# A two-layer table-lookup convolution block on one core: first layer without softmax maxima, lookup over 18 stacks, weights normalised in transposed form, PSUM banks in pairs

## The chip, the cores and the metric

The kernel runs on one core of a Trainium2 chip, in one launch, in fp32 throughout. The metric is device microseconds of one execution; lower is better. The engines are TensorE (PE), VectorE (DVE), ScalarE (ACT), GpSimd (POOL) and SyncE (SP, which only issues DMAs here). Each runs its instructions in the order in which they stand and waits for the others through semaphores.

## The reference

For x of shape (16, 256, 28, 28), a block of pre-activation form is computed. A convolution is replaced here by a soft lookup: each 3x3 patch of a channel (9 numbers) is compared with the channel's 16 centroids, and a softmax over the 16 gives the weights of the centroids' rows in a table.

```python
def amm_conv3x3(x, centroids, w_sub):            # (C,16,9), (C,9,O)
    p = patches(x)                               # B, C, 9 -> p: (b, n, c, 9)
    d = sum(p*p) - 2*einsum('bncs,cks->bnck', p, centroids) + sum(centroids**2)
    attn = softmax(-d, axis=-1)                  # over the 16 centroids
    lut = einsum('cks,cso->cko', centroids, w_sub)
    return einsum('bnck,cko->bno', attn, lut)    # summed over c and k
def block(x):
    out = relu(bn1(amm_conv3x3(x, centroids1, w_sub1)))
    out = bn2(amm_conv3x3(out, centroids2, w_sub2))
    out = se_layer(out)                          # mean over pixels, two small products, sigmoid gate
    return relu(out + x)
y = x + block(groupnorm(x, 32 groups))
```

## The kernel before

**Layout.** The 256 channels are put into 88 rows of 3; 4 such rows fill the 128 partitions of a *stack* (32 partitions each: 27 patch numbers, a row of ones, rows for the maxima), so a layer has 22 stacks (NT), taken in 11 groups of two (NG). The 784 pixels are two tiles of 384 and 400. Layer 1 or 2 of one image is a *stage* of 22 *slots* (11 groups x 2 tiles), and the 32 stages run in the order (1,0) (1,1) (2,0) (1,2) (2,1) ..., so that a stage of layer 1 and one of layer 2 alternate and an image's layer 1 is done a stage ahead of its layer 2. In the code the layers are l = 0 and 1.

**What one group goes through.** Patches of nine shifted copies (`pat`, in DRAM) are loaded to `pt` (L344). PE forms the logits (`lg`, L357: 8 products of 31 rows by 64 columns); DVE transposes them in 32x32 blocks into `z` (L373, 4 banks) and takes the maximum over the 16 centroids (`mx`, L381); for each unit of two groups the maxima are transposed (`mt`, L390) and go through DRAM (`dm`, SP's queue) into spare rows of `pt`. PE then forms the logits a second time, with the maxima subtracted by the product (L357 again), ACT takes the exponential (`e`, L422), and PE multiplies by the centroids (`nm`, L431), which gives the numerators, 9 weighted numbers per channel, and the softmax's sum as one more row. ACT copies these to `q` (L443) and makes 1/sum as exp(-ln(sum)) (`r`, L450 and L451); DVE spreads it to the 9 rows by a stream shuffle (`rb`, L466), POOL multiplies (L467), and PE does the lookup, `q` times the table's rows into two accumulators `acc` of 128 output channels (L475), over all 22 stacks.

**Around it.** When the accumulators of a tile are full, ACT applies the batch norm and writes the layer's image (L491) or `y` (L501). From an image three DRAM copies (`home`, shifted by one column for dx = 0 and 2, with `side` as the shifted image in SBUF, copied by POOL, L271) are written, and from these nine DMAs fill `pat` (L280); all of these are POOL's. A new image is loaded to `xt`, its group statistics are taken on DVE (L222), and POOL normalises it (L253). An image is closed by the gate (two small products, ACT L313 and DVE L316 to L321) and the two halves of `finish` (ACT L330, DVE L331 and L332).

**What sets the order.** Nothing reorders: the program order is written by hand. `at(slot, pos, f, ...)` notes a step, and the steps are emitted sorted by slot, then position 0 to 9. So each engine's order is that of the steps below.

```python
at(s, 0, a_logits, u, gi); at(s, 1, a_turn, u, gi); at(s, 8, a_max, u, gi)
at(s + LB, 5, b_logits, u, gi); at(s + LB, 6, b_exp, u, gi)      # LB = 4
at(s + LN, 3, b_num, u, gi);    at(s + LN, 4, b_keep, u, gi)     # LN = 5
at(s + LN + 1, 0, r_make, u, gi); at(s + LC - 1, 7, c_scale, u, gi)
at(s + LC, 2, c_look, u, gi, 0);  at(s + LC, 7, c_look, u, gi, 1)  # LC = 7
```

PSUM has two accumulator banks and a ring of six single banks (`bank`), each of them [128, 512] fp32, used in turn for logits, numerators and the small products.

Of the kernel before, what the change touches and what calls it, by code (L numbers as in the profile page):

```python
# [15 lines left out]
P = 128  # L16
# [3 lines left out]
K = 16  # L20
NCH = 3
NRT = 88
NT = NRT // 4
NG = NT // 2
CPAD = NRT * NCH
GN_EPS = 1e-5
BN_EPS = 1e-5

# [6 lines left out]
NROW = [r for r in range(32) if r % 8 != 7][:27]  # L35

PXT = ((0, 384, 0, 384), (384, 400, 368, 416))
UNITS = ((0, 2), (2, 2), (4, 2), (6, 2), (8, 2), (10, 1))  # L40


def prow(j, s):
    base, step = PROW[j * 3 + s % 3]
    return base + step * (s // 3)


@with_exitstack
def kernel(
# [11 lines left out]
    sums: bass.AP,  # L61
# [5 lines left out]
):  # L67

# [17 lines left out]
    p_ring = ctx.enter_context(tc.tile_pool(name="p_ring", bufs=6, space=PSUM))  # L86
# [5 lines left out]
    def bank(name):  # L92
        return p_ring.tile([P, 512], F32, tag="ps", name=name)
# [5 lines left out]

    DX = CPAD * NPAD  # L100
    d_home = [dram.tile([3 * CPAD, NPAD], F32, name=f"home{i}") for i in range(2)]
    d_pat = [dram.tile([NRT * 32, HW], F32, name=f"pat{i}") for i in range(3)]
    d_zero = dram.tile([2, NPAD], F32, name="zero")
# [3 lines left out]
    xpool = ctx.enter_context(tc.tile_pool(name="xpool", bufs=2))  # L107

    def load_x(b):
        t = xpool.tile([P, NB, HW], F32, tag="xt", name="xt")  # L110
        nc.gpsimd.dma_start(t, x[b].rearrange("(b p) n -> p b n", p=P))
        xs[b] = t

    xs = {}
    load_x(0)

    def zeros(dims):
        return view(d_zero, 0, dims)  # L120

    def clear_home(i):
        t = d_home[i]
        nc.scalar.dma_start(view(t, 0, [[NPAD, 3 * CPAD], [29 * W, 2], [1, W]]), zeros([[0, 3 * CPAD], [0, 2], [1, W]]))
        nc.scalar.dma_start(view(t, C * NPAD, [[DX, 3], [NPAD, CPAD - C], [1, NPAD]]), zeros([[0, 3], [0, CPAD - C], [1, NPAD]]))

    def clear_pat(i):
        t = d_pat[i]
        nc.scalar.dma_start(view(t, 7 * HW, [[32 * HW, NRT], [8 * HW, 4], [1, HW]]), zeros([[0, NRT], [0, 4], [1, HW]]))
        nc.scalar.dma_start(view(t, ONE * HW, [[32 * HW, NRT], [1, HW]]), view(d_zero, NPAD, [[0, NRT], [1, HW]]))  # L130

    with tc.tile_pool(name="zo", bufs=1) as zpool:
        zo = zpool.tile([2, NPAD], F32, name="zo")
        nc.vector.memset(zo, 1.0)
        nc.vector.memset(zo[0:1], 0.0)
        nc.scalar.dma_start(d_zero, zo)
    clear_home(0)
    clear_pat(0)


    nc.vector.tensor_scalar_mul(gmat, gmat, 1.0 / 8.0)
    mhalf = const.tile([P, NB], F32, name="mhalf")
    nc.vector.memset(mhalf, -0.5)
# [19 lines left out]
    nc.sync.dma_start(b1_sb, se_b1.rearrange("(p o) -> p o", o=1))  # L163
    nb2_sb = const.tile([P, NB], F32, name="nb2_sb")
# [10 lines left out]
    for l in range(2):  # L175
        ga, be, mu, va = (vecs[:, :, 4 * l + i] for i in range(4))
        sc = const.tile([P, NB], F32, name=f"bnsc{l}")
        sh = const.tile([P, NB], F32, name=f"bnsh{l}")
        rsqrt(sc, va, BN_EPS, NB)
        nc.vector.tensor_mul(sc, sc, ga)  # L180
        nc.vector.tensor_mul(sh, mu, sc)
        nc.vector.tensor_sub(sh, be, sh)
        bn.append((sc, sh))


    def setup_codes(l):
        wf = wd[l].rearrange("p t m -> p (t m)")
        n = NT * 64
        for c0 in range(0, n, 416):
            m = min(416, n - c0)  # L190
            sq = tpool.tile([P, 416], F32, tag="z", name="sq")
            nc.gpsimd.tensor_tensor(sq[:, :m], wf[:, c0 : c0 + m], wf[:, c0 : c0 + m], ALU.mult)  # L192
# [12 lines left out]
    for t in mxs:  # L205
        nc.vector.memset(t, 0.0)

    sides = {dx: const.tile([P, NB, HW], F32, name=f"side{dx}") for dx in (0, 2)}
    for t in sides.values():
        nc.gpsimd.memset(t, 0.0)  # L210
# [444 lines left out]
```

## Time and profile before

| | |
|---|---|
| three runs | 4280.79, 4292.75, 4295.6 us (median 4292.75) |
| the profiled execution's own time | 4305.45 us, span 4303.8 us |
| busy, share of the span | PE 95%, DVE 87%, ACT 72%, POOL 52% |
| chain that ended last, by engine | PE 84%, DMA 7%, POOL 4%, DVE 3% |
| DMA | 744.32 MB in 563718 packets, mean 173 GB/s |
| TensorE clock granted | 0.984 |

The profile lists, for the one execution that the hardware profiler recorded, the busy time of each engine, then groups of equal instructions with their total, the mean duration in ns of one, and what ended the idle time ahead of them ("<-PE lg L357": a product of line 357 was waited for). The duration of one instruction includes the time from its start until its result is there, so instructions that follow each other on one engine start closer together than their durations say. 704 slots in the span make some 5.5 to 6 us for each. "The chain that ended last" follows the waits back from the last instruction.

### The profile page before, as it was taken

To read this page: it belongs to the slowest core of one execution; us is meant where nothing else is said; L and a number is where in the kernel's file an instruction comes from. 1 tells how busy PE (TensorE), PEld (TensorE's weight loads), DVE (VectorE), ACT (ScalarE), POOL (GpSimd) and SP (SyncE) were. 2 spreads that over 40 slices of the span, in tenths; PEclk is the share of its full clock that TensorE was granted. 3 is DMA by queue.
4 is the path that set the end of the run, shared out by engine and by line. 5 is a ranking of instruction groups with operands and counts; after the bars stand their busy time and mean duration, and the time that the engine had idled before them with its cause. 6 is when DMAs were issued, how large, how long until landed. Compare 5 with 4: busy or idle time off the path is not lost.

```text
span 4303.8 us, 104911 instructions
## 1 busy us (share of the span) xinstructions
PE 4069.6 (95%) x39696; PEld 1481.4 (34%) x39696; DVE 3761.5 (87%) x9144; ACT 3109.7 (72%) x5905; POOL 2252.7 (52%) x2436
## 2 busy tenths in 40 slices
PE   0899999999999999999999999999999999999998
PEld 0333333333333333333333333333333333333333
DVE  0888998889989989888999989989898889989896
ACT  0467777777777777777777777777777777777677
POOL 2455545555464655545555465554545555455443
PEclk9999999999999999999999999999999999999999
DMA  6654655646465564655646456563655646556532
GB/s 210 207 175 120 209 166 182 191 140 218 132 198 186 181 199 122 197 159 184 199 128 211 151 187 192 171 211 103 209 175 187 193 126 209 159 183 198 168 113 65
DMA packets 563718, 744.32 MB, mean 173 GB/s; under 512 B 419490, under 2 KB 443186, under 8 KB 562956
## 3 DMA queue, kind: packets, MB, share of 16 engines
q0 software_dynamic: 149248, 642.59, 44.3%
q1 hardware_dynamic: 409328, 90.35, 10.1%
q8 instruction: 313, 5.13, 0.5%
q10 hardware_dynamic: 4636, 4.66, 0.4%
q14 instruction: 193, 1.58, 0.1%
HBM read 601.26 MB, written 379.15 MB: 228 GB/s over the span
## 4 chain that ended last, share of the span: by engine, by line
PE 84%; DMA 7%; POOL 4%; DVE 3%; issue 1%; ACT 1%; SPq 0%; ACTq 0%; POOLq 0%; DVEq 0%
PE acc L475 45%; PE lg L357 27%; PE nm L431 12%; DMA dm<-mt 2%; POOL xt L253 2%; DMA pt<-dm 2%; DVE z L373 1%; DMA pat<-home 1%; DMA home<-zero 1%; POOL q L467 1%; DVE mx L381 1%; POOL side L269 1%; ACT e L422 0%; DVE rb L466 0%; DVE y L331 0%
## 5 line engine op out<-in xcount | busy, mean ns | idle before, releaser
L467 POOL TENSOR_TENSOR q<-q,rb 128x384 f32<-128x384 f32 (+1 forms) x1408 | 1404.6, 1015 | 1922.8 <-DVE rb L466 1922.7
L475 PE MATMUL acc<-q,ws 128*128 128x384 f32 (+1 forms) x5632 | 2257.8, 524 | 45.5 <-POOL q L467 44.8
L373 DVE STREAM_TRANSPOSE z<-lg 128x416 f32<-128x416 f32 (+1 forms) x2816 | 1436.8, 568 | 367.8 <-PE lg L357 361.5
L357 PE MATMUL lg<-pt,wd 31*64 31x384 f32 (+2 forms) x22528 | 1392.7, 524 | 98.9 <-DMA pt<-dm 47.3
L475 PEld LDWEIGHTS acc<-q,ws 128*128 128x128 f32 x5632 | 961.2, 190 | 1331.0 <-issue 794.2
L381 DVE TENSOR_REDUCE mx<-z 128x26 f32<-128x416 f32 (+1 forms) x2816 | 1396.9, 561 | 0.0
L422 ACT ACTIVATE e<-lg 128x400 f32<-128x400 f32 (+1 forms) x2816 | 1192.0, 523 | 213.7 <-PE lg L357 212.9
L443 ACT COPY q<-nm 128x384 f32<-128x384 f32 (+1 forms) x1408 | 615.4, 489 | 911.5 <-PE nm L431 904.0
L466 DVE STREAM_SHUFFLE rb<-r 128x384 f32<-128x384 f32 (+1 forms) x1408 | 773.5, 597 | 0.3 <-issue 0.2
L450 ACT ACTIVATE r<-q,srow 128x768 f32<-128x768 f32 (+1 forms) x704 | 755.9, 1074 | 0.0
L357 PEld LDWEIGHTS lg<-pt,wd 31*64 31x64 f32 x22528 | 362.1, 131 | 971.4 <-DVE z L373 480.2
L431 PE MATMUL nm<-e,cw 64*32 64x384 f32 (+1 forms) x11264 | 632.8, 506 | 0.0
L451 ACT ACTIVATE r<-r 128x768 f32<-128x768 f32 (+1 forms) x704 | 603.2, 857 | 22.4
L344 POOL DMA_DIRECT2D pt<-pat x384 | 300.8, 783 | 32.9 <-DMA pat<-home 32.9
L280 POOL DMA_DIRECT2D pat<-home x288 | 245.7, 853 | 37.4 <-DMA pat<-zero 29.3
L431 PEld LDWEIGHTS nm<-e,cw 64*32 64x32 f32 x11264 | 128.0, 105 | 397.9 <-ACT r L451 323.5
L390 DVE STREAM_TRANSPOSE mt<-mx 128x256 f32<-128x256 f32 (+1 forms) x384 | 162.5, 423 | 13.2
L253 POOL TENSOR_SCALAR xt<-xt,gn_gm,gn_rstd 128x784 f32<-128x784 f32 x32 | 95.4, 2984 | 0.1
L194 PE MATMUL sqp<-sq,nhalf_sb 128*128 128x416 f32 (+1 forms) x16 | 9.8, 789 | 62.4 <-POOL sq L192 62.4
L331 DVE SCALAR_TENSOR_TENSOR y<-xt,gn_rstd,y 128x784 f32<-128x784 f32 x32 | 33.2, 1036 | 39.1 <-ACT y L330 38.6
L195 DVE TENSOR_TENSOR wd<-wd,sqp 128x416 f32<-128x416 f32 (+1 forms) x8 | 4.0, 521 | 68.0 <-DMA srow<-in_sums 61.0
L501 ACT ACTIVATE y<-acc,bnsh,bnsc 128x384 f32<-128x384 f32 (+1 forms) x64 | 44.4, 694 | 15.7 <-PE acc L475 15.7
(59 smaller groups left out, 514.7 us busy)
## 6 DMA issues: line engine op xcount, KB each, us to landing
pat<-home POOLq DMA_DIRECT2D x288, 808.5 KB, 6.4
pt<-pat POOLq DMA_DIRECT2D x160, 832.0 KB, 7.7
pt<-pat POOLq DMA_DIRECT2D x160, 768.0 KB, 5.1
home<-side POOLq DMA_DIRECT2D x64, 784.0 KB, 4.2
dm<-mt SPq DMA_DIRECT2D x640, 64.0 KB, 4.2
xt<-in_x POOLq DMA_DIRECT2D x32, 784.0 KB, 6.7
pt<-dm SPq DMA_DIRECT2D x320, 50.0 KB
pt<-dm SPq DMA_DIRECT2D x320, 48.0 KB
```

The lines of the kernel that those rows point to most:

```text
L344: nc.gpsimd.dma_start(pt[:, : 2 * ng, :wn], view(pat_of(u["l"], u["b"]), 2 * g0 * P * HW + wpx, [[HW, P], [P * HW, 2 * ng], [1, wn]]),)
L357: nc.tensor.matmul(bs[i][64 * h : 64 * h + 64, :n], lhsT=wd[l][32 * i : 32 * i + rows, 2 * g + h, :], rhs=u["pt"][32 * i : 32 * i + rows, ...
L373: nc.vector.transpose(z[:, :n], u["lg", gi][i][:, :n])
L381: nc.vector.tensor_reduce(u["mx"][:, 4 * gi + i].rearrange("p (c b) -> p b c", c=2)[:, : n // 32], z[:, :n].rearrange("p (b c k) -> p b c ...
L422: nc.scalar.activation(e[:, :n], bk[:, :n], AF.Exp, scale=2.0)
L431: nc.tensor.matmul(bs[h][32 * i : 32 * i + 32, :n], lhsT=cw[l][64 * h : 64 * h + 64, g, i, :], rhs=e[64 * h : 64 * h + 64, :n], start=True ...
L443: nc.scalar.copy(q[:, h * n : (h + 1) * n], bk[:, :n])
L450: nc.scalar.activation(r[:, : 2 * n], u["q", gi][:, : 2 * n], AF.Ln, scale=srow[:, 0:1], bias=srow[:, 1:2])
L451: nc.scalar.activation(r[:, : 2 * n], r[:, : 2 * n], AF.Exp, scale=-1.0)
L466: nc.vector.stream_shuffle(rb[:, :n], r[:, v], MASK)
L467: nc.gpsimd.tensor_tensor(q[:, v], q[:, v], rb[:, :n], ALU.mult)
L475: nc.tensor.matmul(accs[key][:, :n], lhsT=ws[l][:, 2 * g + h, o * P : (o + 1) * P], rhs=u["q", gi][:, h * n : (h + 1) * n], start=(g == 0 ...
```

## The change

Seven things change together.

1. **Layer 1 without maxima.** Its groups have no first logits, no `z`, `mx`, `mt`, `dm`: the second logits stand alone, with the maxima's rows of `pt` at zero. In return two reductions a group (`ext`, L473 and L474) keep the largest sum and the largest 1/sum; at the end of the program they are compared with a limit of 1e26, the result is read into a register, and behind a branch stands a loop over the images that computes everything again with maxima.
2. **18 stacks in the lookup.** Channel number rt + 84 j stands in row rt, column j. The two groups that come first in a tile (9 and 10, by ORDER) put their weighted numbers, 90 rows, into `qx`; ACT copies five of these per stack into the rows of the sums of the other nine groups (L490), so that the lookup has 36 products of 128 rows in a tile instead of 44, spread over 11 slots by LOOKS.
3. **Normalisation in transposed form.** DVE transposes the numerators from PSUM to `nt` (pixels on the partitions, L466), takes the reciprocal of the three sums per 32 columns (`rc`, L470), POOL multiplies with `rc` read nine times each (L487, L501), and DVE transposes back to `q` (L511). The copies L443, the logarithm and exponential L450 and L451 and the shuffle L466 go.
4. **Paired banks.** Three pairs of banks in turn in place of six banks; transposes, maxima and exponentials each work on a pair, so half as many instructions of twice the size. 400 pixels are transposed as 416 columns each.
5. **No `home`.** Images lie in SBUF with a padding row above and below (`im`, `side`), and 15 smaller DMAs fill `pat` from there in a stage. They are issued by ACT, not POOL.
6. **Moved steps.** Side copies from POOL to ACT (L289, L291), normalisation of the new image from POOL to DVE (L281). One `xt` buffer instead of two; `load_x` one slot ahead of `gn_stats` instead of two; LB 5 (was 4), LC 5 (was 7).
7. **Set-up.** Zeros and ones come as an input instead of being made and written to DRAM, the first image's work comes ahead of the second layer's set-up.

```diff
+    ring = [p_ring.tile([P, 2, 512], F32, name=f"pair{i}") for i in range(3)]
+    def pair():
+        turn[0] += 1
+        return ring[turn[0] % 3]
-    xpool = ctx.enter_context(tc.tile_pool(name="xpool", bufs=2))
+    xpool = ctx.enter_context(tc.tile_pool(name="xpool", bufs=1))
...
     def gn_apply(b):
-            nc.gpsimd.tensor_scalar(
-                xt[:, k], xt[:, k], gm[:, k, 0:1], rstd[:, k : k + 1], op0=ALU.subtract, op1=ALU.mult
+            nc.vector.tensor_scalar(
+                ims[0][:, k, W : W + HW], xt[:, k], gm[:, k, 0:1], rstd[:, k : k + 1], op0=ALU.subtract, op1=ALU.mult
...
-            nc.gpsimd.tensor_copy(to[:, :, 1:W], img[:, :, 0 : W - 1])
+            nc.scalar.copy(to[:, :, 1:W], img[:, :, 0 : W - 1])
...
+    PIECES = [(0, 0, 0, 84, 0), (1, 0, 84, 44, 0), (1, 1, 0, 40, 44), (2, 1, 40, 84, 0), (0, 1, 124, 4, 84)]
+    def to_pat(l, i, pat):
+        dx, (j, k, p0, n, rt) = (1, 0, 2)[i // len(PIECES)], PIECES[i % len(PIECES)]
+        v = (ims[l] if dx == 1 else sides[dx])[p0 : p0 + n, k]
+        nc.scalar.dma_start(
+            view(pat, (32 * rt + base) * HW, [[32 * HW, n], [step * HW, 3], [1, HW]]),
+            bass.AP(v.tensor, v.offset, [list(v.ap[0]), [W, 3], [1, HW]]),
...
     def a_turn(u, gi):
-        for i in range(4):
-            nc.vector.transpose(z[:, :n], u["lg", gi][i][:, :n])
+        for ps in u.pop(("lg", gi)):
+            nc.vector.transpose(z[:, : 64 * nb].rearrange("p (i m) -> p i m", i=2), ps[:, :, : 32 * nb])
...
     def b_exp(u, gi):
-        for bk in u.pop(("lg", gi)):
-            nc.scalar.activation(e[:, :n], bk[:, :n], AF.Exp, scale=2.0)
+        for ps in u.pop(("lg", gi)):
+            nc.scalar.activation(e[:, :, :n], ps[:, :, :n], AF.Exp, scale=2.0)
...
+    def b_turn(u, gi):
+        t = npool.tile([P, 26, 32], F32, tag="nt", name="nt")
+        nc.vector.transpose(
+            t[:, : 2 * nb].rearrange("p (h b) r -> p h (b r)", h=2), u.pop(("nm", gi))[:, :, : 32 * nb])
+        nc.vector.reciprocal(rc[:, : 2 * nb], t[:, : 2 * nb, SUM : SUM + 3])
+        if u["col"][gi] is not None:
+            nc.vector.tensor_reduce(ext[:, 0, col : col + 1], t[:, : 2 * nb, SUM : SUM + 3], axis=AX.XY, op=ALU.max)
+            nc.vector.tensor_reduce(ext[:, 1, col : col + 1], rc[:, : 2 * nb], axis=AX.XY, op=ALU.max)
+    def c_scale(u, gi):
+        if g < NBG:
+            v = t[:, : 2 * nb, :SUM].rearrange("p b (j s) -> p b j s", s=9)
+            nc.gpsimd.tensor_tensor(v, v, rc[:, : 2 * nb].unsqueeze(3).to_broadcast([P, 2 * nb, 3, 9]), ALU.mult)
+            w = qxs[key][:, :nb, 10 * g : 10 * g + 5]
+            nc.scalar.copy(t[:, : 2 * nb].rearrange("p (h b) r -> p h b r", h=2)[:, :, :, SUM:], ...)
...
+    def c_turn(u, gi):
+        nc.vector.transpose(q[:, : 64 * nb], t[:, : 2 * nb].rearrange("p b r -> p (b r)"))
...
+                        if maxed:
+                            at(s - LB, 0, a_logits, u, gi)
+                            at(s - LB, 1, a_turn, u, gi)
+                            at(s - LB, 8, a_max, u, gi)
+                        at(s, 5, b_logits, u, gi)
+                        at(s, 6, b_exp, u, gi)
+                        at(s + 1, 3, b_num, u, gi)
+                        at(s + 1, 4, b_turn, u, gi)
+                        at(s + 1, 4, c_scale, u, gi)
+                        if g < NBG:
+                            at(s + 2, 2, c_turn, u, gi)
...
+                for k, (g, o, h) in enumerate(LOOKS):
+                    s, r = divmod(k * NG, len(LOOKS))
+                    early = maxed and 2 * r < len(LOOKS)
+                    at(n0 + LC + s, 1 if early else 7, c_look, *of[g], o, h)
...
+        def prep(self, l, pat, t, near):
+                    self.at(t + i, 4 + 2 * k, shift, l, dx, k)
+            for i in range(3 * len(PIECES)):
+                self.at(t + 1 + (i // 3 if near else i // 2), 8, to_pat, l, i, pat)
+        def norm(self, b, t):
+            for k, f in enumerate((gn_stats, gn_mean, gn_var, gn_apply)):
+                self.at(t + k, 9, f, b)
+        def close(self, b, ob, te):
+            self.at(te + 1, 9, se_hidden, b)
+            self.at(te + 2, 9, se_gate, b)
+            for k in range(NB):
+                self.at(te + 3 + k, 9, finish, b, k)
...
+        if l == 0 and b >= 1:
+            plan.at(t - NS, 9, load_x, b, x[b])
+            plan.norm(b, t - NS + 1)
+            plan.prep(0, pat_of(0, b), t - NS + 5, False)
+        if l == 1:
+            plan.prep(1, pat_of(1, b), t - NS + (LC + 1 if near else 1), near)
+            plan.at(t + NS + LC, 9, load_x, b, x[b])
+            plan.close(b, out[b], t + NS + LC)
...
+    flag = nc.values_load(bad[0:1, 0:1])
+    with tc.If(flag > 0):
+        with tc.For_i(0, B) as bi:
+            plan.stage(0, "g", d_pat[0], 30, True, [])
+            plan.stage(1, "g", d_pat[1], s1, True, [])
```

How the order moves on three engines. First PE in a slot of layer 1. Before (names: `lg` logits, `acc` lookup, `nm` numerators; 64x416 are first logits, 64x400 second ones):

```order
L357 MATMUL lg<-pt,wd_112 64x416 x8
L475 MATMUL acc_615<-q,ws_116 128x384 x2
L431 MATMUL nm<-e,cw_114 32x400 x8
L357 MATMUL lg<-pt,wd_112 64x400 x8
L475 MATMUL acc_653<-q,ws_116 128x384 x2
```

The same place on PE after the change (`pair` is the bank pair that is written):

```order
L454 MATMUL pair_79<-e,cw_107 32x400 x8
L378 MATMUL pair_80<-pt,wd_105 64x400 x4
L378 MATMUL pair_81<-pt,wd_105 64x400 x4
L522 MATMUL acc_5139<-q,ws_109 128x384
L522 MATMUL acc_5142<-q,ws_109 128x384 x2
```

One set of logits of two is gone, and the lookup, three or four products a slot, stands as a whole behind the logits instead of half of it ahead of the numerators.

DVE in a slot of layer 2 and a bit of the next, before:

```order
L373 STREAM_TRANSPOSE z<-lg 128x384 x4
L466 STREAM_SHUFFLE rb<-r 128x400 x2
L381 TENSOR_REDUCE mx_166<-z 128x12x2 x4
L390 STREAM_TRANSPOSE mt<-mx_166 128x256
L373 STREAM_TRANSPOSE z<-lg 128x384 x4
```

DVE in a slot of layer 2 after it:

```order
L397 STREAM_TRANSPOSE z<-pair_79 128x832
L397 STREAM_TRANSPOSE z<-pair_80 128x832
L511 STREAM_TRANSPOSE q<-nt 128x768
L466 STREAM_TRANSPOSE nt<-pair_81 128x768
L470 RECIPROCAL rc<-nt 128x72
L405 TENSOR_REDUCE mx_142<-z 128x2x13x2 x2
L414 STREAM_TRANSPOSE mt<-mx_142 128x256
```

The two shuffles have given way to two transposes of a pair's size and the reciprocal; `z` and `mx` are half as many, twice as large.

DVE while an image is closed (in a stage of layer 1), before:

```order
L381 TENSOR_REDUCE mx_167<-z 128x12x2 x4
L390 STREAM_TRANSPOSE mt<-mx_167 128x128
L331 SCALAR_TENSOR_TENSOR y<-xt,gn_rstd,y 128x784
L332 SCALAR_TENSOR_TENSOR y<-y,xt 128x784
L373 STREAM_TRANSPOSE z<-lg 128x416 x4
L466 STREAM_SHUFFLE rb<-r 128x384 x2
```

The same steps on DVE after it:

```order
L466 STREAM_TRANSPOSE nt<-pair_79 128x768
L470 RECIPROCAL rc<-nt 128x72
L473 TENSOR_REDUCE ext<-nt 128x1
L474 TENSOR_REDUCE ext<-rc 128x1
L352 SCALAR_TENSOR_TENSOR y<-xt,gn_rstd,y 128x784
L353 SCALAR_TENSOR_TENSOR y<-y,xt 128x784
L511 STREAM_TRANSPOSE q<-nt 128x768
L466 STREAM_TRANSPOSE nt<-pair_79 128x768
```

Behind the two operations of `finish`, which need ACT's `y`, now stand the transposes to `q` and from PSUM; before, first logits' transposes and the shuffles stood there.

ACT at the same place after the change:

```order
L444 ACTIVATE e<-pair_81 128x2x384
L301 DMA pat_83<-side_126 40x3x784
L301 DMA pat_83<-side_126 84x3x784
L351 ACTIVATE y<-y,se_nb,se_gt 128x784
L490 COPY nt<-qx 128x24x5
L444 ACTIVATE e<-pair_80 128x2x384
```

Two pattern DMAs are now issued ahead of `finish`'s half on ACT, and the five-row copy and the exponentials stand behind it.

More of the change, by code (lines that the diff above doesn't have):

```diff
@@ L60 @@
     mones: bass.AP,
-    sums: bass.AP,
+    consts: bass.AP,
     vec: bass.AP,
@@ L290, in se_hidden @@
         _, ysum = ys[b]
-        ps = bank("sep")[:, :1]
+        ps = bank()[:, :1]
         n = 0
```

503 lines of the change are left out of this document (261 added, 242 removed).

## Prediction

> **What bounds the kernel now.** I read the page first (busy time, chain that ended last), then the slot in the middle of the run in order of time, then the groups by shape for prices.
>
> ```profile
> span 4303.8 us, 104911 instructions
> PE 4069.6 (95%) x39696; PEld 1481.4 (34%) x39696; DVE 3761.5 (87%) x9144; ACT 3109.7 (72%) x5905; POOL 2252.7 (52%) x2436
> ...
> PE acc L475 45%; PE lg L357 27%; PE nm L431 12%; DMA dm<-mt 2%; POOL xt L253 2%; DMA pt<-dm 2%; DVE z L373 1%; DMA pat<-home 1%; DMA home<-zero 1%; POOL q L467 1%; DVE mx L381 1%; POOL side L269 1%; ACT e L422 0%; DVE rb L466 0%; DVE y L331 0%
> ```
>
> PE is busy 95% of the span, and three of its lines hold 84% of the chain; DVE at 87% is close behind. One slot in order of time (start, duration, engine, what):
>
> ```profile
> 2005.43 0.95 PE L357 MATMUL lg<-pt,wd 31*64 31x416 f32 x16
> 2006.32 1.56 PE L475 MATMUL acc<-q,ws 128*128 128x384 f32 x4
> 2006.39 2.11 DVE L373 STREAM_TRANSPOSE z<-lg 128x416 f32<-128x416 f32 x4 [0.43 <-PE lg L357]
> 2007.80 0.88 PE L431 MATMUL nm<-e,cw 64*32 64x384 f32 x16
> 2008.43 0.59 DVE L466 STREAM_SHUFFLE rb<-r 128x384 f32<-128x384 f32 x1
> 2008.61 0.90 PE L357 MATMUL lg<-pt,wd 31*64 31x384 f32 x16
> 2009.11 1.96 POOL L467 TENSOR_TENSOR q<-q,rb 128x384 f32<-128x384 f32 x2 [1.95 <-DVE rb L466]
> 2009.40 2.05 DVE L381 TENSOR_REDUCE mx<-z 128x26 f32<-128x416 f32 x4
> 2009.44 1.56 PE L475 MATMUL acc<-q,ws 128*128 128x384 f32 x4
> 2009.57 1.66 ACT L422 ACTIVATE e<-lg 128x384 f32<-128x384 f32 x4
> 2010.93 0.95 PE L357 MATMUL lg<-pt,wd 31*64 31x416 f32 x16
> 2011.49 0.45 DVE L390 STREAM_TRANSPOSE mt<-mx 128x256 f32<-128x256 f32 x1
> ```
>
> PE's starts follow each other without a gap, so a slot costs 5.50 us: first logits 0.89, two look-up calls 1.48, numerators 0.81, second logits 0.83, two look-up calls 1.49. One look-up call (two instructions) is 0.743. DVE fits 4 z (2.04 to the shuffle's start), 2 shuffles, 4 maxima and half an mt into the same 5.5 us: it is almost full too. A handoff between engines is 0.1 us (shuffle ends 2009.02, POOL starts 2009.11). Prices, and bursts where one engine ran unhindered:
>
> ```profile
> L373 DVE STREAM_TRANSPOSE z<-lg 128x384 f32<-128x384 f32 x1408 | 694.8, 551 | 241.5 <-PE lg L357 240.8
> L373 DVE STREAM_TRANSPOSE z<-lg 128x416 f32<-128x416 f32 x1408 | 742.0, 584 | 126.2 <-PE lg L357 120.7
> L381 DVE TENSOR_REDUCE mx<-z 128x24 f32<-128x384 f32 x1408 | 674.9, 545 | 0.0
> L467 POOL TENSOR_TENSOR q<-q,rb 128x384 f32<-128x384 f32 x704 | 690.1, 996 | 936.7 <-DVE rb L466 936.6
> L467 POOL TENSOR_TENSOR q<-q,rb 128x400 f32<-128x400 f32 x704 | 714.5, 1033 | 986.1 <-DVE rb L466 986.1
> L422 ACT ACTIVATE e<-lg 128x384 f32<-128x384 f32 x1408 | 589.8, 515 | 199.5 <-PE lg L357 198.7
> L451 ACT ACTIVATE r<-r 128x768 f32<-128x768 f32 x352 | 296.8, 843 | 11.2
> L443 ACT COPY q<-nm 128x384 f32<-128x384 f32 x704 | 303.0, 482 | 490.1 <-PE nm L431 482.6 <-POOL side L271 5.4
> ...
> 120.55 1.97 DVE L373 STREAM_TRANSPOSE z<-lg 128x384 f32<-128x384 f32 x4
> 122.44 1.89 DVE L381 TENSOR_REDUCE mx<-z 128x24 f32<-128x384 f32 x4
> ```
>
> From the bursts a z of 384 takes (1.97-0.551)/3 = 0.473 from start to start, a maximum (1.89-0.545)/3 = 0.448; 32 more elements add 33 ns, so 1.03 ns each.
>
> **The change, part by part.** *PE.* Layer 1 loses its first logits, and 36 look-up calls over 11 slots replace 44. A 384-pixel slot of layer 1 becomes 0.81+0.83+36/11 x 0.743 = 4.07 us, of layer 2 4.90; at 400 pixels x 400/384, so means of 4.155 and 5.00 against some 5.7 before. If PE set every slot, 352 x 9.155 = 3223 us would do. It will not.
>
> *DVE in layer 2* (352 slots). Two paired z of 768: 2 x (0.473+384 x 1.03 ns) = 1.74; two paired maxima 2 x 0.844 = 1.69; the new numerator transpose, 0.551+0.396 = 0.95 because the reciprocal waits for its end, plus 0.06; the q transpose 0.87; half an mt 0.22; the reciprocal of 72 elements, 0.16 until the next can start. Sum 5.68. Pixels of 400 are transposed as 832: 6.08. Mean 5.88, more than PE's 5.00: DVE becomes the bound, at the pace of a slot before. The two shuffles removed (1.2) are paid back by two longer transposes (1.9). 352 x 5.88 = 2070 us. I charge the q transpose in all 11 slots though 9 have one: without it DVE waits for PE's numerators.
>
> For the reciprocal no such shape is in the trace; the nearest rows:
>
> ```profile
> L491 ACT ACTIVATE h<-acc,bnsh,bnsc 128x384 f32<-128x384 f32 (+1 forms) x64 | 44.5, 695 | 11.9 <-PE acc L475 11.9
> L330 ACT ACTIVATE y<-y,se_nb,se_gt 128x784 f32<-128x784 f32 x32 | 33.8, 1058 | 0.8 <-DVE se_nb L321 0.8
> L331 DVE SCALAR_TENSOR_TENSOR y<-xt,gn_rstd,y 128x784 f32<-128x784 f32 x32 | 33.2, 1036 | 39.1 <-ACT y L330 38.6 <-DMA pt<-pat 0.5
> L222 DVE BATCH_NORM_STATS2 gn_st<-xt 128x6 f32<-128x392 f32 x64 | 32.2, 546 | 0.7 <-DMA xt<-in_x 0.7
> L332 DVE SCALAR_TENSOR_TENSOR y<-y,xt 128x784 f32<-128x784 f32 x32 | 31.2, 975 | 1.1
> L253 POOL TENSOR_SCALAR xt<-xt,gn_gm,gn_rstd 128x784 f32<-128x784 f32 x32 | 95.4, 2984 | 0.1
> L271 POOL COPY side<-h 128x756 f32<-128x756 f32 x32 | 25.4, 831 | 0.0
> L313 ACT ACTIVATE se_gt<-sep,nb_sb 128x1 f32<-128x1 f32 x32 | 6.6, 257 | 5.7 <-PE sep L308 5.7
> L316 DVE TENSOR_SCALAR se_gt<-se_gt 128x2 f32<-128x2 f32 x16 | 2.7, 170 | 11.7 <-ACT se_gt L313 11.7
> L317 DVE RECIPROCAL se_gt<-se_gt 128x2 f32<-128x2 f32 x16 | 2.7, 166 | 0.5
> ...
> 51.30 0.81 ACTq L129 DMA_DIRECT2D pat<-zero  x1
> ...
> xt<-in_x POOLq DMA_DIRECT2D x32, 784.0 KB, 6.7
> ```
>
> RECIPROCAL of 2 elements (166 ns) is no dearer than TENSOR_SCALAR of 2 (170), so I take one step per element, 0.166+70 x 1.03 ns = 0.24; the upper bound is eight steps, 0.166+70 x 8 x 1.03 ns = 0.74. The Trainium skill speaks for that bound: VectorE: DVE Perf Modes, section "First, the fixed hardware budget", has the reciprocal run on iterative-divide operations with a repeat count of 8. Here, 2 elements at eight steps would be 14 ns dearer than the TENSOR_SCALAR; the rows show 4 ns less, so they lean against it, on two elements. By that rule the time would be rival A's.
>
> *Layer 1* (352 slots). Three loops close once per slot. PE: 4.07. ACT: end of the second exponential, half of numerators 0.41, handoff, numerator transpose 0.95, reciprocal issued 0.22 and the watching maximum 0.24 (a small reduction, priced as the reciprocal), handoff, the five-row copy 0.25 until the exponential behind it starts (between 257 ns for one element and 482 for 384), two paired exponentials 0.71+0.84, and 0.3 for handoffs and the start: 3.95. DVE-POOL: numerator transpose 0.95, reciprocal 0.3, handoff, POOL's product, handoff, q transpose 0.87. The product's 648 elements at 2.3 ns (996 to 1033 for 16 more) plus 0.11 make 1.60; the upper bound is the subtract-multiply's 3.8 ns (2984/784), 2.5. I take 1.6, since the strided side copy (831 ns for 756) pays nothing for its strides. Loop 3.9; at 400 pixels 4.2 against PE's 4.24. Three loops within 4%: I take 4.25 per slot, 1496 us.
>
> *New stalls in layer 1.* DVE now stands in the loop, so work placed on it that waits for ACT delays the loop. The closing of an image falls in slots 7 to 9 of a stage in which ACT also issues the pattern DMAs (0.81 each), ahead of the closing work in ACT's order. Gate slot: 2 DMAs, 2 activations of 0.26, 4 small DVE operations of 0.17, then the q transpose: the next numerator transpose starts at 3.7 after the exponentials instead of 0.6, 3.1 lost. First half of finish: 1.62+1.06 on ACT, 1.04+0.98 on DVE, 0.87, handoffs: 5.1 lost; second, with one DMA, 4.3. Two evacuations of 0.695 in a slot with DMAs fill ACT's gap 1.2 too far, and the gate's matmuls add 0.3. 14 us x 15 images = 210. Before, the same waits existed while DVE had slack.
>
> *Moved or nearly free.* 288 pattern and 96 home DMAs leave POOL, and 480 smaller pattern DMAs come to ACT, two a slot in eight slots of a stage, 1.62 us hidden in ACT's gap of 2.0 us between the second exponential and the copy (numerators, transpose, reciprocal); if they took 1.25 instead of 0.81 each, 0.5 us in 8 slots of 16 stages would show, 64 us in layer 1. Each also waits for the DMA eight before it on the queues' shared semaphores; that is four slots, 17 us, against 6.7 us for a load of 784 KB, so I charge none. On SP the maxima's DMAs halve. The side copies move from POOL to ACT (0.83 each): in layer 1's stages the two ahead of an exponential meet slots without a five-row copy, where ACT has 1.1 us to spare; in layer 2's, 32 of them exceed the slack by 0.5: 16. Normalising moves from POOL to DVE: with the statistics already there (4 x 0.5, small ones) and 2 x 0.98 for 784 elements it is 5 us per image in stages where DVE now binds; and x is read one slot after its load rather than two, while it lands after 6.7, 2 more: 15 x 7 = 105. The maxima's round trip through DRAM gets a slot more. The logarithm and second exponential that ACT loses (1.9 a slot) return nothing by themselves: ACT ended no slot before. With three pairs in place of six banks a bank comes free only when its pair has been read; in layer 2 PE has 0.9 us of slack for that, in layer 1 the numerators wait for the same exponentials anyway. The loop through ACT in layer 2, with two look-ups ahead of the numerators (1.49), is 5.4 us, just inside DVE's 5.68; if DVE were faster it would take over.
>
> *Ends.*
>
> ```profile
> 20.00:40.00 20.00, 0.00 (x0) 0.00 (x0) 0.00 (x0) 0.00 (x0) 4.76 (x7) 1.00 0.81 288
> 115.26 5.16 PE L357 MATMUL lg<-pt,wd 31*64 31x384 f32 x40 [39.19 <-DMA pt<-pat]
> 4281.04 1.61 PE L475 MATMUL acc<-q,ws 128*128 128x400 f32 x4
> ```
>
> The first logits started at 115. The intermediate copy in DRAM is gone; about 17 MB (weights, zeros, x, patterns) at 288 GB/s are 59 us, with the patches' load and the chain of the normalisation before it: 75, and 5 for the second layer's setup. From the last look-ups to the end it was 22 us; with five slots of look-ups alone (12) and the check of the watched extremes (3): 37.
>
> Sum: 80+1496+210+2070+105+16+37, and 40 for stage changes (some 1%) = 4054 us, against the profiled 4303.8 (run time 4305.45). The median of the runs shown is 12 less, 4292.75: forecast 4042.
>
> **The rivals.** *A: reciprocal at eight steps.* 7 x 1.03 ns more for each of 70 to 76 elements, 0.53 per slot in layer 2 (187) and, as the loops there have 0.2 to spare at 384 pixels and none at 400, 0.35 in 288 slots of layer 1 (100): 4042+287 = 4329, slower than before. The rows of 2 elements speak against it. It decides from 0.46 us extra per reciprocal on (251 of the 287). Chance 0.12. The sentence of the Trainium skill cited above is this case.
> *B: POOL's product is dear.* Each tenth beyond 1.75 lengthens 288 slots of layer 1; at the bound of 2.5 us, 0.75 x 288 = 216: 4258, still under the time before; only from 2.65, beyond the bound, is it slower. For it speaks that the product's second operand is read with a repeated index, which no row shows; against it the side copy's strides. Chance 0.08.
> *C: the stalls cost little,* since PE fills them with look-ups already due, and the paired operations are cheaper than two singles by more than I count (5.6 per layer-2 slot): 4042-150-100 = 3790. Against it: look-ups are spread evenly, and the per-element price is from a row. Chance 0.17.
> *D: DVE never binds,* layer 2 at PE's 5.00: 4042-310 = 3730. Each of the six long operations would have to be 0.15 shorter than its row allows. Chance 0.03.
> *E: the watch fires* and all is computed again, 16 images of some 115 slots one after the other, at 5 us 9.2 ms more. Worked out from the inputs, layer 1's sums lie between 1.7e-4 and 2.1e10, the limit is 1e26: under 0.01.
>
> **How the numbers follow.** My case 0.6: 3900 to 4180 by the bounds (stalls from half to 1.3 times, product up to 2.0, layer-2 slot 5.7 to 6.1). Slower: A, 0.03 of B and 0.03 of mine: 0.18. Within 0.3% (what a measurement here can tell from no change): 0.04. Faster 0.78. Range 3760 to 4340: it takes in my case, nearly all of B and two thirds of C, and leaves out half of A above and D below, with 0.17 in all.
>
> **What would show it.** PE's share falls to about 80%; DVE about 73% over all, but over 95% in layer-2 stretches, where a slot takes 5.9; layer 1's slots take 4.2 to 4.3, with PE's numerators waiting for ACT. The chain passes from PE to DVE's z and maxima. The finishing operations have long DVE waits for ACT's y. A reciprocal row at 0.24 or 0.74 decides A, POOL's product row at 1.6 or 2.5 decides B. First logits at 75. I am wrong if layer 2 runs at 5.0, or if layer 1 is above 5.

## The result, and the profile after

| | before | after | forecast |
|---|---|---|---|
| median of the runs | 4290.32 us | 4144.21 us (4132.94 to 4152.29) | 4042, range 3760 to 4340 |
| ratio, 95% interval | | 0.966 [0.9631, 0.9689] | 0.942 |
| span of the profiled execution | 4303.8 us | 4141.9 us | |

The change makes the kernel 3.4% faster, 146 us where about 250 were forecast. The page of after, with its chain by engine and by line:

```profile
span 4141.9 us, 81729 instructions
PE 3777.2 (91%) x33042; PEld 1342.1 (32%) x33042; DVE 3244.5 (78%) x4644; ACT 1424.4 (34%) x2385; POOL 1283.7 (31%) x1314
...
PE 44%; DVE 38%; issue 6%; ACT 5%; DMA 4%; ACTq 2%; POOL 0%; DVEq 0%; SPq 0%; POOLq 0%
PE acc L522 20%; PE pair L378 12%; PE pair L454 11%; DVE z L397 9%; DVE nt L466 8%; DVE mx L405 8%; DVE q L511 4%; DVE rc L470 4%; ACT e L444 4%; ACTq L301 2%; DMA pat<-side 2%; DVE mt L414 1%; DMA pt<-dm 1%; DVE y L352 1%; ACT y L351 1%
```

PE's share of the chain has fallen from 84% to 44%, and DVE's `z`, `nt`, `mx`, `q` and `rc` now hold a third of it. One image of the middle cut into stretches (columns: window, its length, then busy time of PE, PEld, DVE, ACT, POOL, the granted clock, DMA share, GB/s): the three slots in which an image is closed; six slots without maxima; eleven with; seven without.

```profile
1984.61:2005.26 20.65, 17.01 (x138) 6.42 (x126) 12.47 (x24) 7.42 (x13) 5.34 (x5) 0.86 0.81 282
2005.26:2031.96 26.70, 25.92 (x222) 9.60 (x228) 15.54 (x30) 11.18 (x18) 12.38 (x14) 0.98 0.35 122
...
2106.09:2175.21 69.12, 64.81 (x604) 21.20 (x600) 67.89 (x82) 23.16 (x39) 18.37 (x18) 1.00 0.60 178
2175.21:2207.34 32.13, 31.80 (x270) 11.73 (x270) 20.93 (x26) 13.12 (x22) 11.94 (x10) 1.00 0.20 57
```

With maxima DVE is busy 67.89 of 69.12 us, 6.28 a slot: it is the bound. Without, a slot takes 4.45 to 4.6, and DVE is busy only 58 to 65% of it, ACT 41 to 42%. PE shows 97 and 99%, but that share counts products that use the engine only in part (see "PE at 80%" below), and the last slots of layer 2 take the same 4.6 whether three or four look-ups fall into them. So no engine is full, and a loop of waits sets the pace; the late copy below tests this. That loop in order of time, 400 pixels, in layer 2's last slots (start, duration, engine, what):

```profile
1944.47 1.05 DVE L466 STREAM_TRANSPOSE nt<-pair 128x832 f32<-128x832 f32 x1 [0.22 <-PE pair L454]
1945.19 2.28 PE L522 MATMUL acc<-q,ws 128*128 128x400 f32 x6
1945.55 0.64 DVE L470 RECIPROCAL rc<-nt 128x78 f32<-128x78 f32 x1
1946.28 0.32 ACT L490 COPY nt<-qx 128x130 f32<-128x130 f32 x1 [2.81 <-DVE rc L470]
1946.37 1.39 POOL L487 TENSOR_TENSOR nt<-nt,rc 128x702 f32<-128x702 f32 x1 [3.19 <-DVE rc L470]
1946.50 1.56 ACT L444 ACTIVATE e<-pair 128x800 f32<-128x800 f32 x2
1947.40 1.59 PE L454 MATMUL pair<-e,cw 64*32 64x400 f32 x16
...
1949.06 1.05 DVE L466 STREAM_TRANSPOSE nt<-pair 128x832 f32<-128x832 f32 x1 [0.23 <-PE pair L454]
```

Numerators' transpose 1.08, reciprocal 0.73 until the copy may start (it overwrites the sums that the reciprocal reads), 0.22 until the exponentials behind it in ACT's order, 1.56 for both, 1.00 for the second half of the numerators: 4.59, over and over. ACT waits 2.81 us for a copy of 0.32 with the next exponentials queued behind it. The prices that the prediction disputed:

```profile
L470 DVE RECIPROCAL rc<-nt 128x72 f32<-128x72 f32 x352 | 212.5, 604 | 12.1
L470 DVE RECIPROCAL rc<-nt 128x78 f32<-128x78 f32 x352 | 226.0, 642 | 12.2
L487 POOL TENSOR_TENSOR nt<-nt,rc 128x648 f32<-128x648 f32 x288 | 373.1, 1295 | 902.7 <-DVE ext L473 505.1 <-DVE rc L470 361.8 <-ACT nt L490 13.6
L281 DVE TENSOR_SCALAR im<-xt,gn_gm,gn_rstd 128x784 f32<-128x784 f32 x32 | 24.3, 801 | 1.2 <-POOL gn_rstd L208 1.2
L352 DVE SCALAR_TENSOR_TENSOR y<-xt,gn_rstd,y 128x784 f32<-128x784 f32 x32 | 33.1, 1034 | 86.1 <-ACT y L351 86.1
```

The reciprocal is 0.60 to 0.64, not 0.24; POOL's product 1.3, not 1.6; `finish` waits 86 us in all for ACT's `y`.

### The profile page after: what moved, and what is told of

It is laid out like the page before. It is cut to its first block, busy times and chain, and to the rows that moved or that the text cites. A ratio compares the mean times of both kernels' runs of the same rounds, so it can differ in the third digit from the quotient of the medians.

```text
span 4141.9 us, 81729 instructions
## 1 busy us (share of the span) xinstructions
PE 3777.2 (91%) x33042; PEld 1342.1 (32%) x33042; DVE 3244.5 (78%) x4644; ACT 1424.4 (34%) x2385; POOL 1283.7 (31%) x1314
## 4 chain that ended last, share of the span: by engine, by line
PE 44%; DVE 38%; issue 6%; ACT 5%; DMA 4%; ACTq 2%; POOL 0%; DVEq 0%; SPq 0%; POOLq 0%
PE acc L522 20%; PE pair L378 12%; PE pair L454 11%; DVE z L397 9%; DVE nt L466 8%; DVE mx L405 8%; DVE q L511 4%; DVE rc L470 4%; ACT e L444 4%; ACTq L301 2%; DMA pat<-side 2%; DVE mt L414 1%; DMA pt<-dm 1%; DVE y L352 1%; ACT y L351 1%
## 5 line engine op out<-in xcount | busy, mean ns | idle before, releaser
L522 PE MATMUL acc<-q,ws 128*128 128x384 f32 (+1 forms) x4608 | 1787.3, 520 | 6.0 <-ACT im L535 6.0
L378 PE MATMUL pair<-pt,wd 31*64 31x400 f32 (+1 forms) x16896 | 1335.2, 521 | 186.0 <-ACT e L444 77.6
L487 POOL TENSOR_TENSOR nt<-nt,rc 128x648 f32<-128x648 f32 (+1 forms) x576 | 773.5, 1343 | 1874.4 <-DVE ext L473 957.2
L444 ACT ACTIVATE e<-pair 128x768 f32<-128x768 f32 (+1 forms) x1408 | 1084.3, 818 | 401.7 <-PE pair L378 390.9
L490 ACT COPY nt<-qx 128x120 f32<-128x120 f32 (+1 forms) x576 | 183.8, 319 | 2216.0 <-DVE rc L470 1145.5
L466 DVE STREAM_TRANSPOSE nt<-pair 128x768 f32<-128x768 f32 (+1 forms) x704 | 701.2, 996 | 283.1 <-PE pair L454 279.5
L454 PE MATMUL pair<-e,cw 64*32 64x384 f32 (+1 forms) x11264 | 791.3, 507 | 131.7 <-ACT e L444 127.9
L511 DVE STREAM_TRANSPOSE q<-nt 128x768 f32<-128x768 f32 (+1 forms) x576 | 569.6, 989 | 331.1 <-POOL nt L487 319.8
L397 DVE STREAM_TRANSPOSE z<-pair 128x768 f32<-128x768 f32 (+1 forms) x704 | 668.8, 985 | 70.4 <-PE pair L378 67.0
L405 DVE TENSOR_REDUCE mx<-z 128x48 f32<-128x768 f32 (+1 forms) x704 | 644.1, 957 | 0.0
L470 DVE RECIPROCAL rc<-nt 128x72 f32<-128x72 f32 (+1 forms) x704 | 438.5, 623 | 24.2
L501 POOL TENSOR_TENSOR qx<-nt,rc 128x324 f32<-128x324 f32 (+3 forms) x256 | 166.2, 668 | 466.5 <-DVE rc L470 339.3
L474 DVE TENSOR_REDUCE ext<-rc 128x1 f32<-128x72 f32 (+1 forms) x352 | 81.4, 231 | 0.0
L289 ACT COPY side<-im 128x756 f32<-128x756 f32 x64 | 52.6, 823 | 35.3 <-DMA pat<-im 35.3
L473 DVE TENSOR_REDUCE ext<-nt 128x1 f32<-128x72 f32 (+1 forms) x352 | 60.7, 173 | 0.0
L291 ACT COPY side<-im 128x756 f32<-128x756 f32 x64 | 52.7, 825 | 7.2 <-DMA pat<-side 7.2
```

Of the source, the lines that this page charges most:

```text
L378: nc.tensor.matmul(ps[i // 2][64 * h : 64 * h + 64, i % 2, :n], lhsT=wd[l][32 * i : 32 * i + rows, 2 * g + h, :], rhs=u["pt"][32 * i : 32 ...
L397: nc.vector.transpose(z[:, : 64 * nb].rearrange("p (i m) -> p i m", i=2), ps[:, :, : 32 * nb])
L405: nc.vector.tensor_reduce(u["mx"][:, a : a + 2].rearrange("p i (c b) -> p i b c", c=2)[:, :, :nb], z[:, : 64 * nb].rearrange("p (i b c k) ...
L444: nc.scalar.activation(e[:, :, :n], ps[:, :, :n], AF.Exp, scale=2.0)
L454: nc.tensor.matmul(ps[32 * i : 32 * i + 32, h, :n], lhsT=cw[l][64 * h : 64 * h + 64, g, i, :], rhs=es[i // 2][64 * h : 64 * h + 64, i % 2, ...
L466: nc.vector.transpose(t[:, : 2 * nb].rearrange("p (h b) r -> p h (b r)", h=2), u.pop(("nm", gi))[:, :, : 32 * nb])
```

## Experiments

The runs were made in three sets, each on one chip beside the kernel before, to which the ratios are. The first set has before without layer 1's maxima, the late copy alone, and layer 2's reciprocal on ACT, without the late copy, or twice on DVE; the last has the pattern DMAs on SP and the runs on the q transpose and on layer 1's reciprocal; the second has the rest. The median of before was 4299, 4286 and 4304 in them (4290 beside after), so a difference of some 20 us between times of two sets is not resolved by the times alone. The slot lengths in the traces then say where it lies.

**Which part gains and which costs.** The first kernel is before, with the steps `a_logits`, `a_turn`, `a_max`, `m_turn`, `m_out` and `m_in` under `if l == 1`. The second is after, with

```diff
-        plan.stage(l, b, pat_of(l, b), t, l == 1, cols if l == 0 else [])
+        plan.stage(l, b, pat_of(l, b), t, True, cols if l == 0 else [])
-    ppool = ctx.enter_context(tc.tile_pool(name="ppool", bufs=5))
+    ppool = ctx.enter_context(tc.tile_pool(name="ppool", bufs=6))
```

> The kernel before with one part of the change alone: layer 1's first logits, their transposes, maxima and round trip are left out, without a watch; all else as before. Theory (the gain is the first logits that leave PE, and the rest of the change gives part of it back): layer-1 slots fall from 5.73 us to PE's 0.81+0.83+4x0.743 = 4.6 at 384 pixels and 4.8 at 400, ACT's 4.4 just under it, so 352 x 1.0 = 350 less: 3940, well under the changed kernel's 4144. Rival (the change needs the new normalisation to profit, since ACT's copy, logarithm and two exponentials become the loop at 5.2 us or more): 4105 or above, about level with the changed kernel.

> The changed kernel with the maxima kept in layer 1 too (and a sixth buffer for the patches, which are then loaded earlier there): all of the change but its first part. Theory (the rest of the change costs more than it returns, since with maxima DVE's work, 6.3 to 6.7 us a slot, is above the 5.5 to 5.7 of a slot before): 704 slots of some 6.5 and 120 at the ends, 4700, slower than before by some 400. Rival (the rest is about neutral against the kernel before, and the first part of the change was cheap): 4300.

Measured: 3899.51 us, ratio 0.9071 [0.9041, 0.9101], and 4844.87 us, 1.1298 [1.1233, 1.1364]. So leaving out layer 1's maxima, without a watch, is worth 9.3% on the old kernel, and the rest of the change together makes that kernel 13% slower. The watch is still in that second kernel; its two reductions take some 0.27 us of DVE a group, so up to 95 us of the 559 that this kernel is slower by are the watch's. The windows of the same eleven slots with maxima and seven without, of the first kernel, and the seven of the second:

```profile
2018.15:2079.98 61.83, 61.54 (x632) 22.19 (x616) 58.11 (x139) 47.91 (x92) 32.02 (x35) 1.00 0.66 205
2079.98:2112.69 32.71, 32.66 (x291) 12.48 (x283) 10.16 (x35) 29.94 (x57) 24.96 (x28) 1.00 0.71 239
```

```profile
2584.29:2628.57 44.28, 41.93 (x387) 13.72 (x382) 43.34 (x54) 13.12 (x22) 11.90 (x10) 1.00 0.30 83
```

In the old form a slot with maxima costs 5.62 (PE full), in the new one 6.28 (DVE full); without maxima it is 4.67 in the old form and 4.59 in the new, although the new one has less work for PE. With maxima in both layers DVE is full in these seven slots too (43.34 of 44.28, 6.33 a slot), and busy 94% of the whole span. The second kernel was 145 us over its expectation: its closing slots, where the 4 us of `finish` come on top for a DVE that has no slack left, take 7.7 to 9.5, together some 7 us an image above three usual ones, 107 in all.

**The loop through ACT.** After, with the five-row copy as a step of its own behind the next group's exponentials:

```diff
+                            at(s + 1, 7, c_copy, u, gi)      # was in c_scale, at (s + 1, 4)
                             at(s + 2, 2, c_turn, u, gi)
```

> The changed kernel with the five-row copy on ACT moved behind the next group's exponentials in both layers (it stood ahead of them). Theory (in slots without maxima the loop is transpose, reciprocal, watch, copy, exponentials, numerators, 4.48 at 384 pixels and 4.68 at 400; without the copy in it PE's 4.07 and 4.24 or the loop of DVE and POOL at 4.1 and 4.3 take over): some 288 slots x 0.35 = 100 less, 4045. Rival (the q transpose, which needs the copy, now comes later and holds up the next numerators' transpose behind it): no gain or slower, 4140 to 4200.

Measured: 3924.56 us, ratio 0.9127 [0.9099, 0.9155], 220 less than after (spans 3922.8 and 4141.9). The theory holds in direction; the size was twice the expectation. Six slots without maxima in layer 1, and the seven of layer 2:

```profile
1892.78:1915.86 23.08, 22.38 (x227) 8.51 (x226) 15.11 (x30) 10.05 (x16) 12.16 (x14) 1.00 0.49 171
...
2058.52:2089.00 30.48, 30.21 (x279) 12.00 (x276) 20.32 (x26) 14.60 (x24) 11.96 (x10) 1.00 0.21 60
```

26.70 became 23.08 and 32.13 became 30.48. In layer 1 the 384-pixel slots fell from 4.5 to 4.0 (I had taken PE's 4.07 as the floor), the first slot of each tile by 1.8, and the three closing slots together by 1.2. The slots with maxima, which the theory had left out, gave another 2.8 an image, some 45 of the 220.

**The reciprocal.** After, with layer 2's on ACT, or done twice on DVE:

```diff
-        nc.vector.reciprocal(rc[:, : 2 * nb], t[:, : 2 * nb, SUM : SUM + 3])
+            nc.scalar.activation(rc[:, : 2 * nb], t[:, : 2 * nb, SUM : SUM + 3], AF.Ln)
+            nc.scalar.activation(rc[:, : 2 * nb], rc[:, : 2 * nb], AF.Exp, scale=-1.0)
```

> The changed kernel, with layer 2's reciprocal made on ACT as exp(-ln(sum)) of the same 72 or 78 elements; layer 1 keeps DVE's. Theory (DVE sets the slots with maxima and the reciprocal's 0.55 us there are all on the path): 352 x 0.55 = 194 less, 3950. Rival (the loop through ACT, which now holds two small operations more ahead of the copy and the exponentials, takes over): under half of it, 4050 or more.

> The changed kernel with layer 2's reciprocal computed twice on DVE (the second into a tile that nobody reads), and at the program's end one reciprocal and one product with a constant for each of 2, 18, 36, 72, 144 and 288 elements per partition. Theory (DVE sets these slots): 352 x 0.55 = 194 more, 4340, and the rows at the end grow by 6.2 ns per element (604 ns at 72 and 166 at 2), six times the product's. Rival of one step per element with a large fixed part: 1 ns per element above some fixed 0.5 us. Rival that DVE has slack there: under 50 more.

Measured: 4045.32 us, ratio 0.9404 [0.9377, 0.943], 99 less; and 4332.47 us, 1.0074 [1.0045, 1.0103], 188 more. Doubling costs what the theory said, though in part for another reason: 0.52 us in each of the 15 slots of an image that have both maxima and layer 2's numerators, as DVE is full there, and 0.49 in the seven of layer 2 without maxima, where DVE is not full but the copy waits for the second reciprocal too.

Removing gives half of it, for two reasons. I counted wrong: the maxima of layer 2 run five slots ahead, so only 15 of an image's 22 slots have both, 15 x 16 x 0.55 = 132 us. And these 15 gave back only 0.29 each; with the copy and the reciprocal both behind the exponentials (the next experiment) they give 0.50, so the rival, the loop through ACT, held the rest. In the seven without maxima ACT's two operations are hardly shorter (0.14 a slot).

Sizes, at the end of the second kernel:

```profile
4300.84 0.16 DVE L671 RECIPROCAL rsz<-ext 128x2 f32<-128x2 f32 x1
...
4301.74 0.38 DVE L671 RECIPROCAL rsz<-ext 128x36 f32<-128x36 f32 x1
...
4302.38 0.60 DVE L671 RECIPROCAL rsz<-ext 128x72 f32<-128x72 f32 x1
...
4304.60 1.95 DVE L671 RECIPROCAL rsz<-ext 128x288 f32<-128x288 f32 x1
4306.59 0.31 DVE L672 TENSOR_SCALAR rsz<-ext 128x288 f32<-128x288 f32 x1
```

(1.95-0.16)/286 = 6.3 ns an element, six times a transpose's 1.03. The row of 2 elements that I had argued from can't show it: 2 x 5.2 ns are lost in the 166 to 170 ns that such small operations take here. The Trainium skill (VectorE: DVE Perf Modes, "First, the fixed hardware budget") gives a repeat count of 8; by these rows an element costs as much as six of a transpose, not eight.

On the kernel with the late copy, layer 2's reciprocal on ACT behind the exponentials (`r_act` at (s + 1, 6.4), `c_scale` at (s + 1, 6.5)):

> The kernel with the late copy (3925), and layer 2's reciprocal on ACT as exp(-ln(sum)), placed behind the exponentials, so that no loop goes through it. Theory (it pays only in the 15 slots of an image that have both maxima and layer 2's numerators, 240 in all, and there in full): 240 x 0.55 = 130 less, 3795. Rival (ACT or POOL's later product closes another loop): half of it or less, 3860 or more.

Measured: 3805.88 us, ratio 0.8871 [0.882, 0.8922], 119 less than with the late copy alone. With the count of 240 slots and no loop through it, it pays nearly in full.

**The closing and the DMAs on ACT.** On the late copy, `finish` cut in two, DVE's part a slot behind ACT's; and on after, the pattern DMAs on SP's queue:

```diff
                 self.at(te + 3 + k, 9, finish, b, k)       # ACT's y only
+                self.at(te + 4 + k, 9, finish2, b, k)      # DVE's two operations
```

```diff
-        nc.scalar.dma_start(                               # in to_pat
+        nc.sync.dma_start(
```

> The kernel with the late copy (3925), and the two DVE operations of each half of the closing moved one slot behind ACT's part. Theory (DVE waits for ACT's y, and the transposes queued behind wait with it): the two closing slots of 8.7 and 6.0 us fall to some 4.5 each against a usual 4.0, 5 to 6 us an image less, 80 in all: 3845. Rival (PE had work in hand, so the time comes back later in the stage): under 20.

> The changed kernel with the pattern DMAs issued from SP's queue instead of ACT's. Theory as forecast (their 0.8 to 0.9 us each lie in ACT's gap between exponentials and copy, save in the closing slots, where two of them stand ahead of ACT's y): 2 to 3 us an image, 40 less, 4105. Rival (they are on the path in all slots that have them): 16 x 30 x 0.3 = 140 less, 4000. Rival (SP's own transfers of the maxima are held up behind them): 4144 or slower.

Measured: 3894.52 us, ratio 0.9077 [0.9025, 0.913], 30 less than with the late copy where 80 were expected (runs 3888.89 to 3895.44 against 3920.99 to 3931.79); and 4110.27 us, 0.9555 [0.9518, 0.9593], 34 less than after. The first compares two sets; by the ratios it is 21, and in the traces layer 1's stage is 2.3 us shorter for each image, 35 in all.

The second meets the forecast's 40 in size, but only in part where the forecast put it. In the traces the gate's slot and that of the first half of `finish` give 1.3 us an image, some 20; layer 2's stages get 0.9 longer each; and 23 of the 34 come from three stages near the ends (the first two and the last but one), which the forecast had not singled out. So the total is partly luck.

Why the first fell short, in its trace:

```profile
1872.25 1.30 POOL L492 TENSOR_TENSOR nt<-nt,rc 128x648 f32<-128x648 f32 x1 [2.69 <-DVE ext L478]
1872.25 2.12 DVE L357 SCALAR_TENSOR_TENSOR y<-xt,gn_rstd,y 128x784 f32<-128x784 f32 x1
...
1874.41 0.98 DVE L358 SCALAR_TENSOR_TENSOR y<-y,xt 128x784 f32<-128x784 f32 x1
1875.30 0.97 DVE L520 STREAM_TRANSPOSE q<-nt 128x768 f32<-128x768 f32 x1
```

Moved behind the watch, `finish` starts together with POOL's product, and takes 2.12 instead of 1.034. The slots that it lengthens are 5.7 instead of the 4.5 expected. Two times 1.1 us an image are some 33 of the missing 50; another 0.8 an image came back in a later slot, why is open.

**All parts, and what was left.** The late copy, the split closing, layer 2's reciprocal on ACT, and `c_turn` at (s + 2, 4.5), behind the next numerators' transpose; that last step alone on the late copy; and the first kernel with layer 1's reciprocal on ACT too.

> The late copy, the split closing, layer 2's reciprocal on ACT behind the exponentials, and the q transpose behind the next numerators' transpose instead of ahead of it. If the parts add up: 3925-80-130-10 = 3705. If one of them takes the cover of another: 3750 to 3800.

> The kernel with the late copy (3925) and the q transpose placed behind the next numerators' transpose. Theory (slots without maxima stand at PE's 4.0 at 384 pixels, and at 400 DVE and POOL's loop of 4.25 is as long as PE's 4.24): 10 less at most, 3915. Rival (that loop still sets the 400-pixel slots, and q gets a whole slot of time): 0.2 x 140 = 30 less, 3895.

> The kernel of all parts (3758) with layer 1's reciprocal on ACT as well, behind the exponentials, and the watch taking the smallest sum instead of the largest reciprocal (so that DVE needn't wait for ACT). Theory (7 slots of each image have maxima of layer 2 beside layer 1's reciprocal, 6.3 to 6.7 us): 16 x 7 x 0.55 = 62 less, 3695. Rival (POOL's product, now later in layer 1's slots, sets them): 3750 or slower.

Measured: 3758.3 us, ratio 0.8765 [0.8712, 0.8818]; 3889.9, 0.9044 [0.9009, 0.9079]; 3758.01, 0.873 [0.8696, 0.8765].

The q transpose gives 35, the rival's size. Its mechanism shows in layer 2's last slots: an even 4.25 with the late copy, they now follow PE, 3.90 with three look-ups and 4.5 to 4.6 with four (some 4.08 in the mean of 36 look-ups in 11 slots, so PE's floor at 400 is below 4.24). But that is only 0.8 us an image, and layer 1's 400-pixel slots got 0.8 longer; the gain lies in layer 1's 384-pixel tile, 2.3 an image, where the theory put none. That the size fits is luck. The parts alone sum to 30+119+35 = 184, together they give 166.

The last kernel is level with the first, not 62 faster: six slots an image with maxima fell by 2.6 us together, five of them by 0.4 to 0.5 as expected, but layer 1's others grew by 1.6, most of it in the fourth (3.3 to 4.8), layer 2's by 0.5, and the six stages at the two ends by some 15 in all. In 14 images the second operation of `finish` now runs beside POOL's product and takes 1.96 instead of 0.98, which can be part of it; no run tests that, and the rest is open.

The version of all parts beats both kernels: 12.4% under before, 9.3% under after.

## Why the prediction was right, and wrong, by its own steps

The direction and the range held. That the total came within 2.5% is partly luck: two rows were 285 us too low together, and the others 197 too high. The terms against what the trace of after shows (slot lengths are distances between starts of `nt`, L466, averaged over the 26 stages of the middle):

| term | forecast | measured |
|---|---|---|
| first logits | 75 | 68.7 |
| 352 slots without maxima | 4.25 each, 1496 | 4.51 each, 1588 |
| closing, 15 images | 14 each, 210 | 7.6 each, 113 |
| 352 slots with maxima | 5.88 each, 2070 | 6.43 each, 2263 |
| new image's normalisation, 15 images | 7 each, 105 | 3.4 each, 51 |
| everything else (second layer's setup, end, stage changes, side copies) | 98 | 58 |
| sum | 4054 | 4142 |

- **DVE becomes the bound with maxima: right.** The mis-sized term was the reciprocal. I took one step per element from a row of 2 elements, and left eight to rival A at 0.12; six is what it is. Of the 0.55 us a slot that were missing, 0.36 are the reciprocal's (0.52 until the next can start, against 0.16). The rest is the watch in the seven of these slots that are layer 1's (0.27 each), the first of them (7.2 us), and DVE's short waits (6.28 a slot against 6.17 busy in the window above).
- **Rival A's mechanism was nearly true, and yet its 4329 is 185 too high, since my case around it was too dear.** It added 287 us; the two rows of slots stand 285 above mine (193+92). Of the 193, 127 are the reciprocal's (352 x 0.36); in the 92 it is one of two terms (next point). But 97 came back at the closing, 54 at the normalisation, 40 in the rest and 6 at the first logits.
- **Layer 1's three loops within 4%: wrong, and it was the loop through ACT that set it.** I had it at 3.95 and PE at 4.07. Missing in my sum were the reciprocal's 0.3 and the second half of the numerators, 1.00 until the transpose instead of 0.41 and a handoff. The late copy showed that no engine was short there: the order of two instructions on ACT cost 220 us, some 175 of it in slots without maxima.
- **The layers are not what separates the slots.** I charged layer 1's and layer 2's 352 each. The sums come out alike, but the trace is cut otherwise: seven of layer 1's slots hold layer 2's maxima, and seven of layer 2's hold none. One experiment (layer 2's reciprocal on ACT) was sized wrong in part through that, not the forecast.
- **Closing: half of what I charged.** The stalls are real (`finish` waits 86 us, and with the late copy moving its part gives 30), but each is smaller than I worked out: the gate's slot is 1.3 above a usual one where I had 3.1, the halves of `finish` 3.6 and 2.8 where I had 5.1 and 4.3, and the 1.5 for evacuations and the gate's products do not show. That the usual slot is 4.5 and not 4.07 is not the reason: with the late copy, at 4.0 a slot, the three still cost 8.0. Why they are smaller stays open. It is on rival C's side, though its second half, cheaper pairs, was not so.
- **Moved DMAs nearly free: right**, 34 us by the run that moves them to SP. **POOL's product: right side**, 1.3 and 1.39 us; rival B is out.
- **Normalisation on DVE:** 0.65 to 0.68 us per 784 elements after the first two images, where I took 0.98.
- **PE at 80%: wrong reading.** It shows 91%, with the same matmuls 3777 us busy here and 3509 in the version of all parts. The difference is in the numerators (791 against 650) and the logits (1335 against 1216). Numerators that come in two halves, each behind its exponential, count 1.59 busy for what takes 0.9 in one piece. In the records the 16 matmuls of one piece start in two rounds of eight, 0.36 us apart; those of two halves start in four rounds of four, each round as long as one of eight. So the busy share counts a round alike, full or half full, and does not tell how much of PE is in use.
- **The gain that was not there.** The median against before was to fall by 250; the first part alone gives 399 on the old kernel. The other parts, the watch among them, cost it 245. In the slots with maxima (5.62 to 6.28 in the windows above) the transposed form moves ACT's slack work onto DVE, which had little slack (58.11 busy of 61.83). In those without, the fewer look-ups gained next to nothing (4.67 to 4.59), as the loop through ACT set the pace; with the late copy they take 4.35.

## What to carry to other kernels

A loop of small waits can bind where DVE, ACT and POOL are no more than 65% busy and PE's share only looks full: follow one slot from a result back to itself, adding start to start, and look for the short instruction that stands ahead of a long one on an in-order engine without needing to. Price an operation from a row of at least the size at hand; a row of two elements shows only the fixed part. And when a change bundles a removal with a rearrangement, cost the removal alone first: here it was worth more than the whole.

## What was not expected of the hardware

- DVE's SCALAR_TENSOR_TENSOR with two inputs in SBUF took 2.12 us when it started with POOL's product (1.30; the split closing), 1.24 when it overlapped the product's last 0.4 (the version of all parts), and 1.03 when nothing of POOL's ran: beside a product it ends 0.83 after the product does; one-input operations are hardly touched: in the version of all parts the q transposes of 768 beside a product took 0.97 (half of them), the others 0.94. The Trainium skill (SBUF — State Buffer, "Terms") has a port pair shared by the two, held for the whole instruction, on which the loser blocks; the rows of SCALAR_TENSOR_TENSOR agree, and the transposes did not block.
- The reciprocal's 6.3 ns an element, against 0.5 for a product with a constant (0.31 us at 288 elements, 0.17 at 2).
